# Cross-attention block on one core: the third pair's tokens loaded as rows and turned on TensorE, its queries and keys moved ahead, and another order in the third step

## The chip, the cores and the metric

The kernel runs on one core of one Trainium2 chip. The metric is the device time of one execution in microseconds (us), the median of the runs shown. A profiled execution has a time of its own and, inside it, a span from its first to its last instruction; all times "at 41.05" below count from the start of that span.

## The reference

All values are float32. `x` and the context `c` are 128 sequences of 128 tokens with 256 features; there are 16 heads of 16 features and a hidden layer of 1024.

```
q = x @ Wq + bq ;  k = c @ Wk + bk ;  v = c @ Wv + bv
scores = q k^T / 4 per head, -1e30 where j >= i        (token i sees only j < i)
attn = softmax(scores), row 0 set to zero
x1   = layer_norm(x + (attn v) @ Wo + bo) * ln1_g + ln1_b
out  = layer_norm(x1 + relu(x1 @ W1 + b1) @ W2 + b2) * ln2_g + ln2_b
```

## The kernel before

**Tiles.** The work goes by pairs of sequences: 64 pairs, each 256 tokens. The order of instructions on every engine is the order in which the program writes them (`tc.manual_schedule` for TensorE = PE, VectorE = DVE, ScalarE = ACT, GpSimd = POOL and SyncE = SP). Each engine takes its instructions in that order, so an instruction that waits holds up all behind it on its engine.

**One pair.** `tokens` turns x and c (features onto partitions) on DVE, from tiles that `load` fetched in 32 x 32 blocks. `queries`, `keys` and `values` are the three projections on PE (`pq`, `pk`, `pv`); ACT takes them out of PSUM (`qT`, four instructions for `kT`, `values_out` for `vz` and `vd`). `scores(p, hi)` makes the scores of the upper (`hi` = 1) or lower 64 rows. The softmax runs over three engines: `mask` and the maxima on DVE, the subtraction on POOL (L353), `exponential` on ACT (L360), the sums and reciprocals on DVE (L372, L373), the multiplication on POOL (L374). The attention weights are then turned: on DVE and by 16 DMAs (`turn`, `bring`, into `pT`), or for the first two pairs on PE (`turn_on_pe`, L417, with ACT copying to `pT`, L419). `weigh` multiplies by the values (`pc`), `context` copies on ACT (L456), `attention_out` is the product with Wo (`po`, L463). Then come `attention_sum` (L489), `attention_stats`, the first layer norm `norm1` (for pair 0 on ACT, L505, for the others on DVE, L509), the turning of its result (`turn_x1` through DRAM; for pair 0 `turn_x1_on_pe`, with ACT applying gain and offset, L632, into `x1T`), `hidden` (`ph`, L647, then ACT, L653, into `hT`), `second` (`py`, L665) and the second layer norm.

**Stages.** A prologue, written out by hand (L745 to L806), starts pairs 0 and 1 and makes the projections of pair 2. Pairs 0 and 1 arrive as rows and are turned on PE (`transposed`, four transposes into one PSUM bank); pair 2 is turned on DVE by `tokens(2, "x")` and `tokens(2, "c")`. Then `step(p)` runs for p = 2 to 62: it works on the scores of pair p, the attention output of p - 1, the projections of p + 1, `hidden` of p - 2 and `second` of p - 3. `step(2)` is special: it has a branch of its own, with `turn_x1_on_pe(0)`, `turn_on_pe` for pair 1, `fold_norm1` (L572, products of the first norm's offset with W1, copied by four ACT instructions, L580), and three quarters of `hidden(0, ...)`; the last quarter stands at its end, followed on ACT by eight of the `bring` DMAs. A last part written out by hand ends pairs 61 to 63.

**Buffers.** All of `pv`, `pq`, `pk`, `po`, `ph`, `py`, `pc` and the transposes on PE share four PSUM banks (`ps_1`); a new one waits until the instructions that read an earlier one in its bank are done. The scores have two tiles of their own.

**Queues.** DMAs are issued from SP (loads, the turning through DRAM, half of `bring`) and from ACT (`vd<-vz` in `values_out`, L302, the other half of `bring`, the stores). Every DMA, of whichever queue, takes the next of eight semaphores in the order in which the program writes them, and its issue waits until the DMA that had that semaphore before has landed. The loads at the start stand in the order `load([2, 3])` (eight block DMAs of 128 KB), `w1` (1 MB), three rows, `w2` (1 MB), `load_tokens(1)`, `load([4, 5])`. The functions that the change touches, and their callers:

Of the kernel before, what the change touches and what calls it, by code (L numbers as in the profile page):

```python
# [13 lines left out]
P = 128  # L14
# [5 lines left out]
def tile_cross_attention_block(  # L20
# [59 lines left out]
    def load(ps, both="xc"):  # L80

        n = len(ps)
        for which in both:
            src = x if which == "x" else c
            t = loads.tile(
                [P, KC, n * 2 * NS, 32], F32, tag=f"{which}b{n}", name=f"{which}b_{ps[0]}",
                bufs=n,
            )
            blocks = src[2 * ps[0] : 2 * ps[0] + 2 * n].rearrange(
                "b (i t) (k j f) -> j t k (b i) f", t=32, k=KC, f=32  # L90
            )
            for j in range(NS):
                nc.sync.dma_start(t[32 * j : 32 * j + 32], blocks[j])
            for u, p in enumerate(ps):
                blocks_of[which, p] = t[:, :, u * 2 * NS : (u + 1) * 2 * NS]

    def load_tokens(g, us=slice(0, 4)):
        if g not in tokens_of:
            tokens_of[g] = loads.tile([P, 4, D], F32, tag="x", name=f"x_{g}", bufs=2)
        nc.sync.dma_start(  # L100
            tokens_of[g][:, us], x[4 * g + us.start : 4 * g + us.stop].rearrange("b p d -> p b d")
        )


    def weight(w, name):
        n = w.shape[0] // P
        t = const.tile([P, n, w.shape[1]], F32, tag=name, name=name)
        nc.sync.dma_start(t, w.rearrange("(k p) n -> p k n", p=P))
        return t
# [11 lines left out]
    def row(v, name):  # L121
        t = const.tile([P, v.shape[1]], F32, tag=name, name=name)
        nc.sync.dma_start(t, v.to_broadcast([P, v.shape[1]]))
        return t
# [22 lines left out]
    b1_c = column(b1, "b1_c")  # L147
    g1_c = chunks(ln1_g, "g1_c")
    be1_c = chunks(ln1_b, "be1_c")
    load([2, 3])  # L150
    w1 = weight(W1, "w1")
    g1_r = row(ln1_g, "g1_r")
    be1_r = row(ln1_b, "be1_r")
    b2_r = row(b2, "b2_r")
    w2 = weight(W2, "w2")
    load_tokens(1)
    load([4, 5])
    g2_r = row(ln2_g, "g2_r")
    be2_r = row(ln2_b, "be2_r")
# [152 lines left out]
    def scores(p, hi):  # L312

        st = states[p]
        n = P if hi else HP
        sps = [pair(f"pss{hi}_{p}_{t}") for t in range(2)]
        for m in range(KC):
            for s in range(2):
                first = s * P
                for r in range(NS):  # L320
                    strip = slice(32 * r, 32 * r + 32)
                    nc.tensor.matmul(  # L322
                        sps[r // 2][
                            s * HP : (s + 1) * HP, r % 2, m * 2 * n : (m + 1) * 2 * n
                        ].rearrange("p (e j) -> p e j", e=2),
                        st["qT"][strip, m, first + hi * HP : first + hi * HP + HP],
                        st["kT"][strip, m, :, first : first + n],
                        start=True, stop=True,
                    )
        st["sps", hi] = sps  # L330
        st["sm", hi] = soft.tile(
            [P, H, n], F32, tag=f"sm{hi}", name=f"sm{hi}_{p}", bufs=2
        )
        st["nmx", hi] = small.tile([P, H], F32, tag=f"nmx{hi}", name=f"nmx{hi}_{p}")

    def mask(p, hi, t):
        st = states[p]
        part = slice(t * HH, (t + 1) * HH)
        n = P if hi else HP
        no = neg.rearrange("p u j -> p (u j)") if hi else neg[:, 1, :]  # L340
        nc.vector.tensor_tensor(  # L341
            st["sm", hi][:, part, :].rearrange("p (r n) j -> p r n j", r=2),
            st["sps", hi][t][:, :, : 4 * n].rearrange("p r (n j) -> p r n j", j=n),
            no[:, None, None, :].to_broadcast([P, 2, 4, n]),
            ALU.add,
        )
# [14 lines left out]

    ALL, ONE, TWO = slice(0, H), slice(0, HH), slice(HH, H)

    def sums(p, hi, part):

        st = states[p]
        sm = st["sm", hi]
        n = sm.shape[2]
        su = small.tile([P, H], F32, tag=f"su{hi}", name=f"su{hi}_{p}_{part.start}")
        rs = small.tile([P, H], F32, tag=f"rs{hi}", name=f"rs{hi}_{p}_{part.start}")  # L370
        su, rs = su[:, part], rs[:, part]
        nc.vector.tensor_reduce(su, sm[:, part, :], AX.X, ALU.add)  # L372
        nc.vector.reciprocal(rs, su)  # L373
        nc.gpsimd.tensor_tensor(  # L374
            sm[:, part, :], sm[:, part, :],
            rs[:, :, None].to_broadcast([P, part.stop - part.start, n]), ALU.mult,
        )
# [392 lines left out]
    ps_bv = fold_values()  # L770
    sums(0, 0, ALL)
    scores(1, 1)
    mask(1, 1, 0)
    maximum(1, 1, ONE)
    turn_on_pe(0, 1, range(2))
    add_values(ps_bv)
    values_out(1)
    turn_on_pe(0, 1, range(2, 4))
    mask(1, 1, 1)
    maximum(1, 1, TWO)  # L780
    add_bo(0)
    turn_on_pe(0, 0, range(2))
    tokens(2, "x")
    scores(1, 0)
    exponential(1, 1, ONE)
    weigh(0)
# [1 line left out]
    mask(1, 0, 0)  # L788
    mask(1, 0, 1)
    maximum(1, 0, ALL)  # L790
    tokens(2, "c")
    attention_out(0)
    exponential(1, 1, TWO)
    sums(1, 1, ONE)
    attention_sum(0)
    attention_stats(0)
    shift(0, 1)
    exponential(1, 0, ALL)
    queries(2)
    sums(1, 1, TWO)  # L800
    keys(2)
    norm1(0)
    sums(1, 0, ALL)
    nc.gpsimd.tensor_tensor(be1b_r, be1_r, b2_r, ALU.add)
    values(2)
    values_out(2)  # L806
# [14 lines left out]
    def step(p):  # L821
        nonlocal waiting
        if p > 2:
            load_ahead(p)
        scores(p, 1)
        mask(p, 1, 0)
        maximum(p, 1, ONE)
        if p > 2:
            second(p - 3, 0)
            mask(p, 1, 1)  # L830
            maximum(p, 1, TWO)
            exponential(p, 1, ONE)
            second(p - 3, 1)
            if p + 2 < NP:
                tokens(p + 2, "c")
        else:
            turn_x1_on_pe(0)
            turn_on_pe(1, 1, range(2))
            fold_norm1()
            add_b1()  # L840
            hidden(0, range(FC // 2))
            mask(p, 1, 1)
            maximum(p, 1, TWO)
            exponential(p, 1, ONE)
            low_scores(p)
            turn_on_pe(1, 1, range(2, 4))
            hidden(0, range(FC // 2, 3 * FC // 4))
            turn_on_pe(1, 0, range(2))
            tokens(3, "x")
            add_bo(1)  # L850
        summed = []
        sums(p, 1, ONE)
        exponential(p, 1, TWO)
        if p > 2:
            second_sum(p - 3)
            summed = [p - 3]
        else:
            tokens(3, "c")
            load_ahead(2)
            load_tokens(2)  # L860
            exponential(p, 0, ALL)
        sums(p, 1, TWO)


        weigh(p - 1)
        context(p - 1)
        if p > 2:
            scores(p, 0)
        if p == 3:
            scale_w1()  # L870
            nc.gpsimd.tensor_tensor(b1e_c, b1e_c, b1_c, ALU.add)
        queries(p + 1)
        if p > 2:
            mask(p, 0, 0)
            mask(p, 0, 1)
            maximum(p, 0, ALL)
        if p > 2:
            exponential(p, 0, ALL)
        else:
            sums(p, 0, ALL)  # L880
            add_bo(2)
        turn(p, 1, 0)
        turn(p, 1, 1)
        for q in waiting:
            finish(q)
        attention_out(p - 1)
        attention_sum(p - 1)
        if p > 2:
            sums(p, 0, ALL)
        else:  # L890
            turn(p, 0, 0)
            bring(p, nc.sync, range(NS * NS // 2))
        attention_stats(p - 1)
        if p + 2 < NP:
            tokens(p + 2, "x")
            if p == 2:
                tokens(p + 2, "c")
        if p > 2:
            turn(p, 0, 0)
            bring(p, nc.sync, range(NS * NS // 2))  # L900
        keys(p + 1)
        norm1(p - 1)
        turn_x1(p - 1)
        values(p + 1)
        values_out(p + 1)
        for q in waiting:
            store(q)
        add_bo(p + 1)
        if p == 2:
            residual1(0)  # L910
        residual1(p - 1)
        for q in summed:
            stats(q, states[q]["t2"], 2)
        for q in summed:
            scale_and_shift(q)
        at = NS * NS // 2

        def share(f):
            nonlocal at
            n = NS * NS - at if f == FC - 2 else 0 if f == 0 or p == 2 else NS // 2  # L920
            bring(p, nc.scalar, range(at, at + n))
            at += n

        hidden(p - 2, range(0 if p > 2 else 3 * FC // 4, FC), share)
        for q in summed:
            norm2(q)
        waiting = summed
# [129 lines left out]
```

## Time and profile before

| | |
|---|---|
| median of 3 runs | 1587.57 us (1587.35 to 1588.86) |
| the profiled execution | 1587.7 us |
| its span | 1585.9 us |
| granted TensorE clock, mean | 0.999 |
| busy PE / DVE / POOL / ACT | 99% / 86% / 81% / 48% |
| steady step | 24.27 us (`py` of one step at 112.07, of the next at 136.34) |

How to read it: in a line of the timeline the first number is the start, the second the time from the first start to the last end of the group, then engine, source line, operation, output<-input, shape and count; the brackets give how long the engine idled just before it and what ended that. "SPq" and "ACTq" are DMA issues. Starts are a better measure than durations for PE, since its matmuls overlap: the time a group takes is the distance from its start to the next group's start. Times from the kernel's start to 80 us are the part in which the change lies.

### The profile page before, as it was taken

What the parts mean: (1) busy time and instruction counts of PE and PEld (TensorE: products, weight loads), DVE (VectorE), ACT (ScalarE), POOL (GpSimd) and SP (SyncE); (2) the same over time, 40 slices, a digit from 0 to 9 for tenths busy, and PEclk for the clock granted to TensorE, in tenths of its full rate; (3) what the DMA queues carried; (4) which work ended last, traced back from release to release, by engine and by line L of the source; (5) the groups of instructions that cost most, each with busy time, mean ns of one, the idle gap of its engine ahead of it and who ended that gap; (6) DMA issues with size and microseconds to landing.
All of it is one profiled execution on the core that took longest, in us unless ns stands there. A gap on an engine that the chain in (4) does not pass through costs nothing.

```text
span 1585.9 us, 41280 instructions
## 1 busy us (share of the span) xinstructions
PE 1573.9 (99%) x16514; PEld 1329.4 (84%) x16514; DVE 1369.9 (86%) x1989; ACT 756.8 (48%) x1500; POOL 1281.4 (81%) x1105
## 2 busy tenths in 40 slices
PE   8999999999999999999999999999999999999998
PEld 7788888888888888888888888888888888888887
DVE  7899888888888988898898988888889888889872
ACT  5555445444444454444444444544444455445442
POOL 7878888788887888888888888878888888888883
PEclk9999999999999999999999999999999999999999
DMA  9555665755656556566566565565555655654521
GB/s 199 112 132 127 150 143 121 148 125 133 147 123 144 140 124 159 134 125 147 126 139 146 124 141 138 120 158 130 138 134 126 152 145 123 143 138 108 127 78 34
DMA packets 479935, 210.12 MB, mean 132 GB/s; under 512 B 348672, under 2 KB 448256, under 8 KB 479744
## 3 DMA queue, kind: packets, MB, share of 16 engines
q1 hardware_dynamic: 371104, 134.29, 38.8%
q10 hardware_dynamic: 108640, 73.19, 18.0%
q8 instruction: 131, 2.15, 0.6%
q14 instruction: 60, 0.49, 0.1%
HBM read 70.00 MB, written 33.03 MB: 65 GB/s over the span
## 4 chain that ended last, share of the span: by engine, by line
PE 95%; DMA 1%; DVE 1%; POOL 1%; ACT 1%; SPq 1%; issue 0%; ACTq 0%; POOLq 0%; DVEq 0%
PE ph L647 28%; PE py L665 27%; PE pq L256 7%; PE po L463 7%; PE pk L256 7%; PE pv L288 7%; PE pss L322 6%; PE pc L444 4%; PE pc L434 2%; DMA pT<-tb 1%; SPq L402 0%; POOL sm L374 0%; PE ptp L417 0%; DMA x1t<-tbx 0%; DVE sm L341 0%
## 5 line engine op out<-in xcount | busy, mean ns | idle before, releaser
L353 POOL TENSOR_TENSOR sm<-sm,nmx 128x1024 f32<-128x1024 f32 x192 | 364.3, 1898 | 119.8 <-DVE nmx L352 116.6
L647 PE MATMUL ph<-x1T,w 128*128 128x256 f32 x2048 | 453.4, 380 | 0.0
L665 PE MATMUL py<-w,hT 128*128 128x256 f32 x2016 | 452.8, 383 | 0.3 <-ACT hT L653 0.3
L665 PEld LDWEIGHTS py<-w,hT 128*128 128x128 f32 x2016 | 378.3, 190 | 72.7 <-issue 19.6
L374 POOL TENSOR_TENSOR sm<-sm,rs 128x1024 f32<-128x1024 f32 x192 | 364.2, 1898 | 89.8 <-DVE rs L373 86.2
L647 PEld LDWEIGHTS ph<-x1T,w 128*128 128x128 f32 x2048 | 389.5, 190 | 52.7 <-ACT x1T L632 0.5
L653 ACT ACTIVATE hT<-ph,b1e_c 128x256 f32<-128x256 f32 x504 | 208.6, 471 | 203.0 <-PE ph L647 103.4
L360 ACT ACTIVATE sm<-sm 128x1024 f32<-128x1024 f32 x192 | 200.9, 1054 | 203.9 <-POOL sm L353 203.6
L372 DVE TENSOR_REDUCE su<-sm 128x8 f32<-128x1024 f32 (+1 forms) x192 | 233.6, 1217 | 68.8 <-ACT sm L360 66.7
L341 DVE TENSOR_TENSOR sm<-pss,neg 128x1024 f32<-128x1024 f32 (+1 forms) x256 | 235.1, 939 | 52.4 <-PE pss L322 51.0
L387 DVE STREAM_TRANSPOSE tb<-sm 128x1024 f32<-128x1024 f32 x183 | 220.0, 1227 | 27.9 <-POOL sm L374 27.8
L352 DVE TENSOR_REDUCE nmx<-sm 128x8 f32<-128x1024 f32 (+1 forms) x192 | 234.2, 1220 | 6.6
L542 ACT ACTIVATE t<-t,nb,sd 128x256 f32<-128x256 f32 x124 | 67.7, 593 | 192.3 <-DMA pT<-tb 110.7
L256 PE MATMUL pq<-xT,wq 128*128 128x256 f32 x504 | 125.5, 392 | 0.0
L278 ACT ACTIVATE kT<-pk,bkh,half 128x256 f32<-128x256 f32 x252 | 120.6, 558 | 3.5 <-PE pk L256 3.5
L463 PE MATMUL po<-wo,cxT 128*128 128x256 f32 x512 | 121.1, 380 | 0.7 <-ACT cxT L456 0.7
L288 PE MATMUL pv<-wv,cT 128*128 128x256 f32 x512 | 121.0, 379 | 0.0
L256 PE MATMUL pk<-cT,wk 128*128 128x256 f32 x504 | 119.2, 380 | 0.0
L322 PE MATMUL pss<-kT,qT 32*64 32x256 f32 (+1 forms) x4096 | 116.2, 334 | 0.0
L517 POOL TENSOR_TENSOR x1b<-x,g_r 128x512 f32<-128x512 f32 x64 | 81.5, 1274 | 34.8 <-DVE x L509 34.8
L463 PEld LDWEIGHTS po<-wo,cxT 128*128 128x128 f32 x512 | 97.3, 190 | 13.9 <-ACT cxT L456 0.8
L288 PEld LDWEIGHTS pv<-wv,cT 128*128 128x128 f32 x512 | 97.4, 190 | 13.0
(99 smaller groups left out, 1718.9 us busy)
## 6 DMA issues: line engine op xcount, KB each, us to landing
pT<-tb SPq DMA_DIRECT2D x488, 96.0 KB, 2.9
pT<-tb ACTq DMA_DIRECT2D x488, 96.0 KB, 2.7
out_dram<-t ACTq DMA_DIRECT2D x63, 256.0 KB, 2.5
xb<-in_x_dram SPq DMA_DIRECT2D x124, 128.0 KB, 4.5
cb<-in_ctx_dram SPq DMA_DIRECT2D x124, 128.0 KB, 4.5
x<-in_x_dram SPq DMA_DIRECT2D x31, 512.0 KB, 5.5
x1t<-tbx SPq DMA_DIRECT2D x248, 64.0 KB, 2.3
x1T<-x1t SPq DMA_DIRECT2D x62, 256.0 KB, 3.1
```

The lines of the kernel that those rows point to most:

```text
L256: nc.tensor.matmul(ps[:, m * TP : (m + 1) * TP], w[:, k, m * P : (m + 1) * P], src[:, k, :], start=(k == 0), stop=(k == KC - 1),)
L288: nc.tensor.matmul(pv[:, s * D : (s + 1) * D], st["cT"][:, k, s * P : (s + 1) * P], wv[:, k, :], start=(k == 0), stop=(k == KC - 1),)
L322: nc.tensor.matmul(sps[r // 2][s * HP : (s + 1) * HP, r % 2, m * 2 * n : (m + 1) * 2 * n].rearrange("p (e j) -> p e j", e=2), st["qT"][str ...
L341: nc.vector.tensor_tensor(st["sm", hi][:, part, :].rearrange("p (r n) j -> p r n j", r=2), st["sps", hi][t][:, :, : 4 * n].rearrange("p r ...
L352: nc.vector.tensor_reduce(nmx[:, part], sm[:, part, :], AX.X, ALU.max, negate=True)
L353: nc.gpsimd.tensor_tensor(sm[:, part, :], sm[:, part, :], nmx[:, part, None].to_broadcast([P, part.stop - part.start, n]), ALU.add,)
L372: nc.vector.tensor_reduce(su, sm[:, part, :], AX.X, ALU.add)
L374: nc.gpsimd.tensor_tensor(sm[:, part, :], sm[:, part, :], rs[:, :, None].to_broadcast([P, part.stop - part.start, n]), ALU.mult,)
L387: nc.vector.transpose(st["tb"][:, :, at : at + 256].rearrange("p j (n a) -> p n j a", a=32), st["sm", hi].rearrange("p h j -> p (h j)")[:, ...
L463: nc.tensor.matmul(po[:, s * D : (s + 1) * D], cxT[:, k, s, :], wo[:, k, :], start=(k == 0), stop=(k == KC - 1),)
L647: nc.tensor.matmul(ph[:, i * TP : (i + 1) * TP].rearrange("p (s i a) -> p s i a", s=2, a=32), w1[:, k, (f + i) * P : (f + i + 1) * P], st[ ...
L665: nc.tensor.matmul(st["py"][:, s * D : (s + 1) * D], st["hT"][:, f, s * P : (s + 1) * P], w2[:, f, :], start=(f == 0), stop=(f == FC - 1),)
```

## The change

Pair 2's tokens come as rows (x into `tokens_of[1][:, 0:2]`, c into the new tile `c_third`) and are turned by `turned_on_pe`: four transposes on PE each, and one ACT copy each; the two `tokens(2, ...)` on DVE go. `load([2, 3])` becomes `load([3])`, eight block DMAs of 64 KB, and now stands behind `w1`; its tiles have a tag of their own. `queries(2)` moves between the two halves of `turn_on_pe(0, 1, ...)`; `keys(2)` moves ahead of `attention_out(0)`. `sums` is split so that the DVE part of `sums(1, 1, TWO)` stands ahead of `attention_sum(0)` while its POOL part (`divide`) stays where it was: POOL's order does not change. `exponential(1, 0, ALL)` moves ahead on ACT. In `step(2)` `turn_x1_on_pe(0)` goes behind `turn_on_pe(1, 1, range(2))` and `fold_norm1`; `hidden(0, range(4))` is split in two around `low_scores`, and two of pair 1's transposes move ahead of the third part of `hidden`. From `step(3)` on the order of every engine is that of before.

```diff
-    load([2, 3])
+    load_tokens(1, slice(0, 2))
+    c_third = const.tile([P, 2, D], F32, tag="c_third", name="c_third")
+    nc.sync.dma_start(c_third, c[4:6].rearrange("b p d -> p b d"))
     w1 = weight(W1, "w1")
+    load([3])
...
-    load_tokens(1)
+    load_tokens(1, slice(2, 4))
     load([4, 5])
...
-    def sums(p, hi, part):
+    def sums(p, hi, part, then=True):
...
         nc.vector.tensor_reduce(su, sm[:, part, :], AX.X, ALU.add)
         nc.vector.reciprocal(rs, su)
+        if then:
+            divide(p, hi, part, rs)
+        return rs
+
+    def divide(p, hi, part, rs):
+        sm = states[p]["sm", hi]
+        n = sm.shape[2]
         nc.gpsimd.tensor_tensor(
...
     scores(1, 1)
+
+    def turned_on_pe(p, which, src):
+        st = states.setdefault(p, {})
+        st[which + "T"] = proj.tile([P, KC, TP], F32, tag=which + "T", name=f"{which}T_{p}")
+        pt = transposed(src, f"pt{which}_{p}")
+        nc.scalar.copy(st[which + "T"].rearrange("p k i -> p (k i)"), pt)
+
+    turned_on_pe(2, "x", tokens_of[1][:, 0:2])
     mask(1, 1, 0)
     maximum(1, 1, ONE)
     turn_on_pe(0, 1, range(2))
     add_values(ps_bv)
     values_out(1)
+    turned_on_pe(2, "c", c_third)
+    queries(2)
     turn_on_pe(0, 1, range(2, 4))
     mask(1, 1, 1)
     maximum(1, 1, TWO)
     add_bo(0)
     turn_on_pe(0, 0, range(2))
-    tokens(2, "x")
     scores(1, 0)
     exponential(1, 1, ONE)
     weigh(0)
...
     maximum(1, 0, ALL)
-    tokens(2, "c")
+    exponential(1, 1, TWO)
+    keys(2)
     attention_out(0)
-    exponential(1, 1, TWO)
     sums(1, 1, ONE)
+    rs_two = sums(1, 1, TWO, then=False)
+    exponential(1, 0, ALL)
     attention_sum(0)
     attention_stats(0)
     shift(0, 1)
-    exponential(1, 0, ALL)
-    queries(2)
-    sums(1, 1, TWO)
-    keys(2)
+    divide(1, 1, TWO, rs_two)
+    sums(1, 0, ALL)
     norm1(0)
-    sums(1, 0, ALL)
...
-            turn_x1_on_pe(0)
             turn_on_pe(1, 1, range(2))
             fold_norm1()
             add_b1()
-            hidden(0, range(FC // 2))
+            turn_x1_on_pe(0)
+            hidden(0, range(FC // 4))
             mask(p, 1, 1)
             maximum(p, 1, TWO)
             exponential(p, 1, ONE)
             low_scores(p)
+            hidden(0, range(FC // 4, FC // 2))
             turn_on_pe(1, 1, range(2, 4))
+            turn_on_pe(1, 0, range(2))
             hidden(0, range(FC // 2, 3 * FC // 4))
-            turn_on_pe(1, 0, range(2))
```

## The prediction

> **What bounds the kernel now.** The page comes first: its span, and the share of each engine.
>
> ```profile
> span 1585.9 us, 41280 instructions
> ...
> PE 1573.9 (99%) x16514; PEld 1329.4 (84%) x16514; DVE 1369.9 (86%) x1989; ACT 756.8 (48%) x1500; POOL 1281.4 (81%) x1105
> ```
>
> PE is the bound, and it stands still for only 12.0 us in all. The windows tell where (length, then busy time of PE, PEld, DVE, ACT, POOL, then the granted clock, DMA share, GB/s):
>
> ```profile
> 20.00:80.00 60.00, 55.77 (x718) 44.91 (x717) 53.46 (x71) 36.91 (x72) 52.02 (x37) 1.00 0.68 143
> 80.00:200.00 120.00, 120.00 (x1275) 101.49 (x1274) 108.25 (x156) 58.62 (x116) 98.71 (x84) 1.00 0.61 134
> 200.00:1500.00 1300.00, 1299.11 (x13651) 1098.37 (x13650) 1151.26 (x1661) 620.68 (x1234) 1069.69 (x914) 1.00 0.59 136
> ```
>
> From 80 us to 1500 PE is busy 1419.1 of 1420.0 us, and from `step(3)` on the change leaves every engine's order as it was. So what PE gains or loses before about 73 us moves the whole rest, and nothing else counts. The waits of PE between 20 and 80 us (us in total, times, longest) are what can be won:
>
> ```profile
> PE ptp L417 <- POOL sm L374: 1.8, 3, 0.8
> PE pc L434 <- DMA x1t<-tbx: 0.8, 1, 0.8
> PE pc L434 <- ACT pT L419: 0.7, 2, 0.5
> PE po L463 <- ACT cxT L456: 0.7, 1, 0.7
> ```
>
> By the timeline they stand at 23.23, 25.09 and 26.95 (0.32 + 0.76 + 0.77), 31.08 (0.68), 50.79 and 51.28 (0.53 + 0.18) and 70.64 (0.84): 4.08 us. The name DMA x1t at 70.64 hides the landing of pair 2's last `pT` DMAs.
>
> **What is added to PE.** Eight transposes. Their price is that of the same form for pair 1:
>
> ```profile
> 11.56 0.66 PE L222 MATMUL ptx<-ident,x 128*128 128x128 f32 x4
> 12.05 0.60 PE L222 MATMUL ptc<-ident,c_first 128*128 128x128 f32 x4
> 12.49 1.89 PE L288 MATMUL pv<-wv,cT 128*128 128x256 f32 x8
> ```
>
> From start to start four take 0.49 and 0.44 us: 0.93 for eight. So the most that can be won is 4.08 - 0.93 = 3.15 us, 0.20% of the time. That is just under 0.2%, 3.2 us, which is about what a measurement of this kernel can tell from no change.
>
> **To the product with Wo.** Between `scores(1, 1)` (21.80) and `po` of pair 0, PE now also does the eight transposes (0.93), `pq` (32.91 to 34.64: 1.73) and `pk` (34.64 to 36.37: 1.73): 4.39 us more, against 2.53 us of waits there. With every wait filled `po` would start at 31.08 + 4.39 - 2.53 = 32.94. But new waits come. All these tiles share four PSUM banks, and ACT empties each: the second pair of `ptp` needs the copy of x (done about 24.3), `pq` the first `pT` copy; four further transposes (0.88) then go through before their `pT` copies (two take 0.94 to 0.95, at 26.79 and 41.97) are done, so `weigh(0)` waits about 0.5. I take 1.0 us for these together: `po` at 33.93, 2.85 later than before. Ends: 0 (all banks free in time) and 1.9 (each of four handovers waiting a whole 0.48 us copy).
>
> **From there to `hidden`.** Now `pv` follows `po` directly: PE is ready for what follows 2.85 - 3.46 = 0.61 us earlier than before. But t1 (the sum with x, on DVE) waits for `po`. Before, `po` started at 31.08 and `x1` on ACT at 38.38; DVE's two sums of pair 1 and the statistics lie between, and POOL's order holds a part of it, so of the 2.85 I take 1.0 through: `x1` at 39.4. Ends: 0 (DVE and POOL were the bound, not `po`) and 2.85. ACT's timeline of before shows what follows:
>
> ```profile
> 38.38 1.10 ACT L505 ACTIVATE x<-t,nb,sd 128x256 f32<-128x256 f32 x2
> 39.36 0.65 ACT L298 COPY vz<-pv 128x256 f32<-128x256 f32 x2
> 40.04 0.60 ACTq L302 DMA_DIRECT2D vd<-vz  x1
> 40.68 0.36 ACT L303 COPY vd<-pv 64x256 f32<-64x256 f32 x1 [0.67 <-ACT vz L298]
> 41.05 1.02 ACT L632 ACTIVATE x1T<-ptn,be_c,g_c 128x256 f32<-128x256 f32 x2
> 41.97 1.07 ACT L419 COPY pT<-ptp 128x512 f32<-128x512 f32 x2
> 42.91 1.52 ACT L580 COPY b1s<-ps_b 1x256 f32<-1x256 f32 x4
> 44.45 0.84 ACT L653 ACTIVATE hT<-ph,b_c 128x256 f32<-128x256 f32 x2
> ```
>
> This is the step that decides. ACT is never idle here. From `x1` to `x1T` it takes 2.67 us (38.38 to 41.05), and PE got its first `ph` at 42.29. In the new order the `pT` copies (0.94) and the four `b1s` (1.54) stand ahead of `x1T`: 39.4 + 2.67 + 0.94 + 1.54 = 44.5, the first `x1T` is done some 0.6 later (two take 1.02), and `ph` starts at 45.1, 2.8 us later than before. `turn_x1_on_pe` was put behind `fold_norm1` on PE, which is cheap there, but its reader on ACT went behind that too. PE meanwhile has `ptp`, the 16 products of `fold_norm1` (41.10 to 42.29) and `ptn` (0.5), and idles about 1.25 us ahead of `ptn`, which waits for ACT's `vd` copy to free its bank, and 2.5 us ahead of `ph`.
>
> **To the end of the change.** From the first `ph` PE's work is the same as before, less waits: 0.53 + 0.18 at 51 us go, as pair 1's transposes have moved ahead of a part of `hidden`; `weigh(1)`, 1.95 us from its start at 50.79 to the end of its `pc`, is then back at the 1.49 of `weigh(2)` (70.64 to 72.13), of which 0.18 is the wait counted, so 0.28; and 0.84 at 70.64 goes if the `pT` DMAs are in time. Their second half is issued on ACT behind the last `hT`: before, the last `ph` started at 59.75 and the last of these landed at 69.27, 9.5 later, while SP's issues had to wait for ACT's landings. Now the last `ph` starts about 61.5, so they land by 71.1, and `py`, which takes 7.1 us, ends at about 71.6. This is close; a DMA that takes 3.15 instead of 2.15 us (both are seen there) brings back up to 0.8. Sum: 2.8 - 0.71 - 0.28 - 0.84 = **+1.0 us**. Ends: -2.5 (`x1T` not late at all: 2.8 becomes -0.6) and +4.6 (1.9 for the banks instead of 1.0, all 3.75 of it through to `x1`, so `ph` 1.8 + 3.75 later, and the 0.84 at 70.64 as before: 5.55 - 0.71 - 0.28).
>
> **What costs nothing.** DVE loses two stream transposes of 0.70 us (28.59 and 31.64), and has waits of 1.12 us at 39.38 and 2.46 at 46.71 anyway; its sums of the second half, moved ahead of t1, take 1.4 us and are in the 1.0 above. The rows of x and c are issued at 8.1 and 8.6 in place of the block loads and are wanted at 22.9 and 24.7. The 64 KB blocks of `load([3])` now stand on SP behind `w1`; DVE reads them at 49.2 and 51.2. `w1` itself comes earlier (issued at about 9.1, before at 16.24) and is wanted at 39. `load([4, 5])` and the second half of x move earlier with them.
>
> **Rivals.** *A load in the way of ACT (slower).* Eight semaphores go round over all queues. In the new order the `vd<-vz` of pair 0 on ACT (L302, issued at 15.19) gets the semaphore of the first block of `load([3])`, which on SP stands behind `w1`. Before, the issue of `w1` (SP's timeline) and its time from issue to landing (the DMA view) were:
>
> ```profile
> 16.24 0.74 SPq L108 DMA_DIRECT2D w<-in_L_xattn_W_dram  x1
> ```
>
> ```profile
> w<-in_L_xattn_W_dram SPq DMA_DIRECT2D x1, 1024.0 KB, 7.0
> ```
>
> `w2`, issued at 18.55 among other loads, took 10.2. Loads on SP landed in their order (`w1` 23.20, `w2` 28.75, x 31.35). With 7.0 `w1` lands at 16.1 and the block about 1 us later, near 17.2; ACT has 0.56 us of waiting at 18.57 and 0.45 elsewhere there, so this is nearly free. From 17 on each us is a us, since `kT` of pair 1 (done 21.35) releases `scores(1, 1)` at 21.80. With 10.2 it is 19.3 + 1.2 = 20.5: +3.5 us, in all 1588.6 + 3.5 = 1592.1. Against it: at 9 us few other loads are under way, which is nearer to the 7.0.
>
> *The clock falls.* PE now idles 1.25 and 2.5 us with only 0.5 us of transposes between. The Trainium skill ("TensorE: Matmul & The Clock Gate", What's actually happening) has the clock at half after an idle window of some 3.4 us, and says (Part 4: PE-mode transpose) that transposes do not count as busy; that speaks against this change. The windows at both ends of the trace, same columns:
>
> ```profile
> 3.66:7.07 3.41, 3.33 (x13) 2.50 (x12) 1.41 (x3) 0.16 (x1) 2.85 (x5) 1.00 1.00 311
> ...
> 1584.03:1585.90 1.87, 0.00 (x0) 0.00 (x0) 0.00 (x0) 0.00 (x0) 0.00 (x0) 0.50 0.20 70
> ```
>
> PE's last matmul ended at 1580.56, and the record falls to half at 1584.03, 3.47 us on. In the first line PE did almost only transposes; ones before 7 us took 0.23 each from start to start, later ones 0.11 to 0.12, so they warmed it, or did not stop its warming. A longest single gap of 2.5 us stays under 3.47, so I take no fall. If it falls: at the start PE went at half its later rate from 1.44 to 7.07, 5.6 us, and half of as much is lost again, 2.8 us, in all 1591.4.
>
> *The waits are filled (faster).* `x1T` comes in time, for instance because `x1` is ready much earlier: -2.5 to -3.15 us, 1585.1 to 1584.5, still within 0.2%. Against it stands the order on ACT, which the trace shows without idle time.
>
> **How the numbers follow.** The profiled execution took 1587.7 us, 0.1 above the median of 1587.57; the change is put on the median: 1587.6 + 1.0 = 1588.6. Chances: forecast 0.75 (alone mostly 1586.2 to 1590.8), load in the way 0.13, clock 0.06, waits filled 0.06. The range leaves out the far parts of the last three: 1586.0 to 1591.6. Faster by over 0.2% needs all of 4.08 us filled and a little more: 0.03. Slower by over 0.2% (above 1590.8): most of the load and the clock rivals and the upper end of the forecast: 0.18. Within: 0.79.
>
> **What would show it.** Right: `po` near 33.9, `x1T` behind `b1s` on ACT near 44.5, a wait of 2 to 3 us at the first `ph` released by L632, no wait at 51, the next step's scores of the lower rows at 73.1 (72.13 before). Wrong: an ACT gap at 15 to 20 us at L302 with `scores(1, 1)` past 22; matmuls of `ph` at twice their distance near 45; `ph` at 42.

## The result, and the profile after

The changed kernel takes 1596.85 us (median; 1593.75 to 1598.53) against 1588.21 for the kernel before in the same session: slower by 0.49%, ratio 1.0049 (95% interval 1.0039 to 1.0060). The forecast was 1588.6, and its range ended at 1591.6. The profiled execution took 1598.53 us, the longest of the six, so what is read from it explains that execution and not the median. Its page, answering to the lines of before:

```profile
span 1596.8 us, 41299 instructions
...
PE 1579.3 (99%) x16522; PEld 1330.2 (83%) x16522; DVE 1367.8 (86%) x1987; ACT 756.2 (47%) x1502; POOL 1281.5 (80%) x1105
```

The span is 10.9 us longer, and PE is busy 5.4 us more, although only eight transposes (0.93) were added: some of its work ran slower. The windows say where (second number PE, third from the end the granted clock):

```profile
20.00:80.00 60.00, 51.74 (x563) 39.67 (x561) 43.39 (x56) 33.69 (x69) 43.45 (x32) 0.91 0.58 109
80.00:200.00 120.00, 119.41 (x1271) 100.87 (x1271) 107.12 (x156) 59.62 (x118) 98.18 (x85) 1.00 0.59 138
200.00:1500.00 1300.00, 1298.91 (x13741) 1096.75 (x13740) 1152.11 (x1658) 620.09 (x1229) 1070.37 (x907) 1.00 0.59 135
```

From 20 to 80 us PE loses 8.3 us to waits (4.2 before), and the clock, 1.00 before, is 0.91 on the mean; from 200 to 1500 us PE is as busy as before (1298.91 and 1299.11). The waits of PE in the first 90 us, the costliest first:

```profile
PE ph L657 <- ACT x1T L642: 2.3, 1, 2.3
PE pk L259 <- issue: 2.3, 1, 2.3
PE pss L325 <- ACT kT L281: 1.6, 2, 1.4
...
PE ptn L225 <- ACT vd L306: 1.3, 1, 1.3
PE pc L444 <- issue: 0.4, 1, 0.4
```

The first and the fourth were forecast (2.5 and 1.25). The second and third were not in the sum. PE's timeline (the products alone) and ACT's show what they do:

```profile
33.69 0.48 PE L259 MATMUL pk<-cT,wk 128*128 128x256 f32 x1
36.47 3.27 PE L259 MATMUL pk<-cT,wk 128*128 128x256 f32 x7 [2.30 <-issue]
39.58 1.89 PE L473 MATMUL po<-wo,cxT 128*128 128x256 f32 x8
...
50.68 3.78 PE L657 MATMUL ph<-x1T,w 128*128 128x256 f32 x8 [2.31 <-ACT x1T L642]
```

```profile
14.21 0.65 ACT L301 COPY vz<-pv 128x256 f32<-128x256 f32 x2 [1.15 <-PE pv L291]
18.31 0.73 ACTq L305 DMA_DIRECT2D vd<-vz  x1
19.09 0.36 ACT L306 COPY vd<-pv 64x256 f32<-64x256 f32 x1 [4.23 <-POOL sm L356]
...
45.01 1.09 ACT L515 ACTIVATE x<-t,nb,sd 128x256 f32<-128x256 f32 x2 [2.35 <-POOL nb L538]
46.01 0.62 ACT L301 COPY vz<-pv 128x256 f32<-128x256 f32 x2
46.66 0.60 ACTq L305 DMA_DIRECT2D vd<-vz  x1
47.30 0.36 ACT L306 COPY vd<-pv 64x256 f32<-64x256 f32 x1 [0.67 <-ACT vz L301]
47.57 1.06 ACT L429 COPY pT<-ptp 128x512 f32<-128x512 f32 x2
48.52 1.52 ACT L590 COPY b1s<-ps_b 1x256 f32<-1x256 f32 x4
50.07 1.02 ACT L642 ACTIVATE x1T<-ptn,be_c,g_c 128x256 f32<-128x256 f32 x2
```

Three things are to be seen. ACT sits at L305 from 14.9 to 18.3: the first rival of the prediction. (The profile names POOL's L356 for the idle time, but `vd` waits for no such thing; the first block of `load([3])`, issued at 9.46, is what the issue waited for, as the runs with that load moved show.) Seven products of `pk` take 3.11 us to the start of `po`, against 1.73 for eight at full clock, and eight of `ph` 3.71. And from `x1` to `x1T` ACT takes 5.06 us, as forecast (5.15). The windows of 3.41 us round the slow stretches:

```profile
32.76:36.17 3.41, 1.41 (x71) 1.02 (x59) 3.27 (x5) 1.91 (x3) 3.41 (x4) 0.99 0.75 111
36.17:39.58 3.41, 3.11 (x8) 2.52 (x8) 0.77 (x2) 0.00 (x0) 1.88 (x2) 0.51 0.94 145
...
46.40:49.81 3.41, 0.72 (x8) 0.42 (x4) 3.15 (x3) 2.67 (x8) 3.41 (x4) 0.99 0.22 38
49.81:53.22 3.41, 2.54 (x6) 2.09 (x7) 0.00 (x0) 1.25 (x3) 3.41 (x2) 0.50 0.15 13
53.22:56.63 3.41, 3.41 (x38) 2.16 (x38) 1.00 (x2) 1.78 (x3) 0.10 (x1) 0.50 0.96 145
```

The clock is at half for one such window from 36.1 and for two from 49.8, each time after a window in which PE was busy less than half the time. All edges lie on one grid of 3.41 us; they stand some 0.05 us earlier than these windows, and by them the two windows before the falls hold 1.46 and 0.76 us of work.

### The profile page after: what moved, and what is told of

Same layout as the page of the kernel before. It is cut to its first block, busy times and chain, and to the rows that moved or that the text cites. A ratio compares the mean times of both kernels' runs of the same rounds, so it can differ in the third digit from the quotient of the medians.

```text
span 1596.8 us, 41299 instructions
## 1 busy us (share of the span) xinstructions
PE 1579.3 (99%) x16522; PEld 1330.2 (83%) x16522; DVE 1367.8 (86%) x1987; ACT 756.2 (47%) x1502; POOL 1281.5 (80%) x1105
## 4 chain that ended last, share of the span: by engine, by line
PE 93%; DVE 2%; DMA 1%; ACT 1%; SPq 1%; POOL 1%; issue 1%; ACTq 0%; POOLq 0%; DVEq 0%
PE ph L657 27%; PE py L675 26%; PE pq L259 7%; PE po L473 7%; PE pk L259 7%; PE pv L291 6%; PE pss L325 6%; PE pc L454 3%; PE pc L444 2%; DMA pT<-tb 1%; SPq L412 1%; DVE su L375 0%; DVE sm L344 0%; DVE nmx L355 0%; ACT sm L363 0%
## 5 line engine op out<-in xcount | busy, mean ns | idle before, releaser
L356 POOL TENSOR_TENSOR sm<-sm,nmx 128x1024 f32<-128x1024 f32 x192 | 364.2, 1897 | 116.2 <-DVE nmx L355 116.0
L259 PEld LDWEIGHTS pk<-cT,wk 128*128 128x128 f32 x504 | 96.5, 192 | 16.1 <-issue 2.8
```

Source lines behind the costliest of these rows:

```text
L259: nc.tensor.matmul(ps[:, m * TP : (m + 1) * TP], w[:, k, m * P : (m + 1) * P], src[:, k, :], start=(k == 0), stop=(k == KC - 1),)
L356: nc.gpsimd.tensor_tensor(sm[:, part, :], sm[:, part, :], nmx[:, part, None].to_broadcast([P, part.stop - part.start, n]), ALU.add,)
```

## The experiments

The start of the kernel scatters from run to run: the first `pk` takes 1.83 us in most profiles, but 2.1 to 2.4 in before, cover and best2, and 3.6 in ring, fill and quiet. So places are counted from pair 1's first transposes (11.56 in before, 11.29 in after). The last column is where the change ends. The profiles late and quiet are left out, since in them a later wait of PE (6.18 and 9.30 us) falls into the stretch.

| profile | scores(1,1) | gap at `pk` | `po` | first `ph` | `ph` to end | scores(3,0) |
|---|---|---|---|---|---|---|
| before | 10.24 | 0 | 19.52 | 30.73 | 29.84 | 60.57 |
| after | 11.75 | 2.30 | 28.29 | 39.39 | 31.47 | 70.86 |
| after2 | 11.35 | 2.29 | 27.93 | 39.16 | 31.53 | 70.69 |
| ring | 10.24 | 0 | 22.26 | 33.36 | 30.27 | 63.63 |
| fill | 10.24 | 0.90 | 23.42 | 34.53 | 28.69 | 63.22 |
| x1f | 11.42 | 0.54 | 24.72 | 34.05 | 28.60 | 62.65 |
| both | 10.24 | 0.44 | 22.95 | 32.29 | 28.68 | 60.97 |
| cover | 10.24 | 0.63 | 23.67 | 33.01 | 28.69 | 61.69 |
| ringfill | 10.24 | 1.15 | 23.67 | 34.78 | 28.66 | 63.44 |
| step2_only | 10.24 | 0 | 19.53 | 32.62 | 28.98 | 61.60 |
| best2 | 10.24 | 0.53 | 23.05 | 31.80 | 28.69 | 60.49 |
| best3 | 10.24 | 0.33 | 23.37 | 32.12 | 28.66 | 60.78 |

**Blocks ahead of w1 (ring).**

```diff
-    w1 = weight(W1, "w1")
     load([3])
+    w1 = weight(W1, "w1")
```

> Theory: the vd<-vz of pair 0 on ACT waits for the landing of the first block of load([3]), which stands behind w1. With load([3]) ahead of w1 that block lands near 13, the issue goes out near 15 (18.31 in the changed kernel), kT of pair 1 is done near 21.4 and scores(1, 1) start near 21.8 instead of 23.04: 1.7 us less on PE, all else as in the changed kernel, 1595.1. Rival: kT of pair 1 is late for another reason (the exponentials behind POOL), scores(1, 1) stay at 23 and the time at 1596.8.

1592.77 us, ratio 1.0033 (1.0021 to 1.0045). scores(1,1) is back at 10.24, and the gap at `pk` is gone too, which was not expected; the run's start was 1.8 us late, though, so that ACT might not have met the wait in any case (fill, with after's load order and the same late start, did not). The runs both, ringfill and best2 with their ordinary starts settle it: the issue goes out at 14.6 to 15.5 and scores(1,1) never wait. This trace also holds the forecast's own order nearly alone: `po` 2.74 us later than before (forecast 2.85), `ph` 2.63 (forecast 2.8). The clock still fell, for one window:

```profile
46.78 2.66 PE L657 MATMUL ph<-x1T,w 128*128 128x256 f32 x8 [2.31 <-ACT x1T L642]
```

**Loads of pairs 4 and 5 late (late).**

```diff
-    load([4, 5])
...
             add_b1()
+            load([4, 5])
```

> Theory: the 2.30 us at 34.17 in which PE waits for nothing shown is its own instruction fetch, held up by the eight 128 KB block DMAs of load([4, 5]), and the half clock after it comes from that gap. With load([4, 5]) issued only behind add_b1 (near 47) the DMA engines are quiet at 33: no such gap, no half clock at 36, 2.3 + 1.6 = 3.9 us less, 1592.9. Rival: the gap comes of the instructions themselves (so many short ones ahead of it), whatever the DMA engines do: it stays, 1596.8; pair 4's blocks may then only be later.

1600.72 us, ratio 1.0080 (1.0067 to 1.0093). The late loads push the next ones (`xb` of pairs 6 and 7, 55.6 to 72.2 on SP) ahead of pair 2's `pT`, and PE waits 6.18 us at `weigh(2)`. The gap at `pk` was 0.82 and the clock did not fall there, but the other versions, with those loads in place, had 0.33 to 1.15, so this run says neither. At that time `w2` and x were still under way.

**The waits filled (fill).**

```diff
+            pf = pair("pf"); fillers(pf, 0, 3)
             turn_x1_on_pe(0)
+            fillers(pf, 1, 5)
```

> Three extra products (into a free PSUM tile, used for nothing) ahead of the transposes of x1 and five behind them fill the two waits of PE (1.26 and 2.31 us). Theory: the half clock from 49.8 to 56.6 comes of these waits; with PE busy the clock stays full there, ph of pair 0 goes at its usual distance, 3.0 us less: 1593.8. The waits themselves stay, since x1T comes when it did. Rival: the clock falls for another reason (it goes on from the fall at 36, or transposes): 1596.8 and half clock near 50 as before.

1595.15 us, ratio 1.0046 (1.0033 to 1.0058); the profiled execution took 1593.56. The clock is full throughout, and with products in both waits `ph` goes at its usual distance:

```profile
47.74 2.02 PE L657 MATMUL ph<-x1T,w 128*128 128x256 f32 x8
```

From `ph` to the end it is 28.69 us against 31.47: 2.8 us is what the second fall cost. The whole gained only 1.7 by the medians, 0.5 by the ratios, where 3.0 were expected; the trace has a further wait of PE for nothing shown (0.64 at the next `pq`), which the extra instructions may have brought.

**x1 turned first again (x1f).**

```diff
+            turn_x1_on_pe(0)
             turn_on_pe(1, 1, range(2))
             fold_norm1()
             add_b1()
-            turn_x1_on_pe(0)
```

> turn_x1_on_pe(0) back at the head of step 2, all else as changed. Theory: the order on ACT (two pT copies and four b1s copies ahead of x1T) makes x1T 2.5 us late and with it the first ph; that wait goes, and the half clock after it (3.0): 5.5 us less, 1591.3. Rival: x1T is late because x1 is, behind po; then ph moves by less than 0.5 us and the time stays near 1596.

1590.82 us, ratio 1.0021 (1.0012 to 1.0030): 6.0 us less than the changed kernel by the medians, 4.4 by the ratios (0.28% of 1588), 5.5 expected. That it came near is in part luck: by the traces scores(3,0) come 8.21 us earlier, but 3.57 of them stand ahead of `po`, where the edit changes no order (a smaller gap at `pk`, and no fall of the clock there); 4.64 lie behind it. There is no wait ahead of `ph` and no fall; PE waits 1.4 us for `x1` instead, ahead of `ptn`. The order on ACT was the cause, not `x1`.

**Both edits (both).**

> load([3]) ahead of w1 and turn_x1_on_pe(0) back at the head of step 2. Theory: beyond the order itself three costs were left out of the forecast: ACT's wait for the first block (1.3 to 1.7), PE's wait for its own instructions (0.5 to 2.3, gone in the run with load([3]) ahead of w1, where the instruction fetch was recorded 17.1 us after pair 1's first transposes instead of 20 to 22.5), and the half clock. None is left here; the run with the order alone undone stood at +2.1 us by the trace, less 1.3 and 0.5: +0.2 us on before, 1587.8. Rival: the wait for instructions depends on PE's order alone and stays; then +0.8 or more and a gap at the second product of pk.

1590.22 us, ratio 1.0013 (1.0004 to 1.0021); the profiled execution, 1588.23, stands at +0.40 by the trace. The ACT wait is gone, the clock full, but 0.44 us of the gap at `pk` stayed, as the rival had it: the loads' order alone does not remove it. The median lies 2.4 us above the expectation, and the trace does not show why.

**The forecast's own case (ringfill).** ring and fill together.

> load([3]) ahead of w1, and the eight extra products that keep PE busy through its two waits, the changed order kept. This is what the forecast had: new order, no ACT wait at L305, full clock. Theory: +1.0 of the forecast and 0.4 for the pT that come late at weigh(2): +1.4 us on before, 1589.0, with ph of pair 0 starting 2.6 to 2.8 us later than before, counted from pair 1's first transposes. Rival: the order itself costs more than the sum says; then over +2.5 us with full clock and no gap at pk.

1594.26 us, ratio 1.0043 (1.0029 to 1.0056): a miss by 5 us, so that no run shows the forecast's case as a time. Up to the end of the change the trace is as the theory has it but for the gap, 1.15 us: `ph` +4.05 (2.8 + 1.15 = 3.95), scores(3,0) +2.87. Yet the span is 6.6 us longer than before's. Of what comes later, 0.68 is a wait at `pq` as in fill, and from 90 to 1480 us PE stands idle 2.5 us instead of 0.9. The rest was not found. So a kernel with extra instructions is no clean measure of the whole time here; its trace up to 75 us is.

**The third step alone (step2_only).** The prologue of before with the changed branch of `step(2)`.

> The prologue of before with the third step of the changed kernel. Theory: x1T stands behind pT and b1s on ACT, 1.9 to 2.5 us late; later waits give 1.4 back: +0.5 us with a full clock; with a gap of some 2.3 us ahead of ph the clock falls for one or two windows of 3.4 us and takes 1.7 to 3.0 more: +2.2 to +3.5, 1589.8 to 1591.1. Rival: the fall of the clock needs the prologue's shorter or longer waits too; then full clock and 1588.1.

1589.20 us, ratio 1.0011 (1.0002 to 1.0020), from 1587.63 (the profiled one) to 1593.45. `ph` came 1.89 us later, 0.86 was given back, scores(3,0) +1.03. In this profile the clock stayed full though PE waited 2.06 us ahead of `ph`; so a gap of this size does not always make it fall. The gap (41.53 to 43.59) was cut by an edge of the grid at 42.16, and the window behind that edge still held 1.99 us of work.

**A quiet start (quiet).** Both edits, with `w2`, half of x, `load([4, 5])` and two rows behind `add_b1`.

> As both edits together (load([3]) ahead of w1, turn_x1 at the head of step 2), with w2, the second half of x, load([4, 5]) and two rows issued only behind add_b1, so that the DMA engines are idle from about 25 to 45 us; only the profile up to pair 1's weigh is read, later these loads are in the way. Theory: PE's wait for its instructions (0.44 us there, at the second product of pk) is an instruction fetch that starts when PE has done some 214 matmuls and is late behind queued loads; with quiet engines it is recorded at most 0.5 us after that point and the gap is gone. Rival: the fetch is not held up by loads; its time and the gap stay.

No gap at `pk`; the single time, 1603.02, holds a later wait of 9.3 us for `pT`. The time at which PE's instruction fetch (queue q8 in the DMA view) is recorded fits all profiles. The view does not name the engine: q8 has 131 packets in a run, one for every 252 of PE's 16522 matmuls and as many weight loads, and that it is PE's is read from this. In quiet and ring the fetch comes 0.3 us after PE's 214th matmul; take that as the point where it is asked for. The fetches of the changed kernel (33.8 to 33.9) and of quiet (30.5 to 30.6):

```profile
q8 instruction: 1, 0.02, 65.1%
```

```profile
q8 instruction: 1, 0.02, 59.6%
```

| profile | 214th matmul | fetch | 345th (two ahead of `pk`) | gap ends |
|---|---|---|---|---|
| before | 28.2 | 31.4 | 34.2 | no gap |
| after | 30.3 | 33.8 | 33.5 | 36.47 |
| after2 | 29.8 | 33.0 | 33.1 | 36.03 |
| x1f | 29.9 | 31.2 | 33.2 | 34.39 |
| both | 28.0 | 29.3 | 31.3 | 32.34 |
| late | 29.4 | 31.3 | 32.7 | 34.18 |
| quiet | 30.2 | 30.5 | 33.5 | no gap |
| ring | 30.4 | 30.7 | 33.7 | no gap |

The gap always ends 2.5 to 3.2 us after the recorded fetch, and always at the second product of `pk`; the later waits at `pq` in fill and ringfill end 2.7 and 2.5 us after a fetch too. Before, PE took 6.1 us from the 214th matmul to the 345th; in the new order, where only transposes, scores and `weigh` lie between, 3.3. Before had a fetch late by 3.2 us and hid it, with less than 1 us to spare. So the shorter stretch is what laid the wait open. That the wait is for the fetch is argued from these times; no run removed the fetch alone. Why the fetch is late by 0.3 in ring and by 1.3 and 1.9 in both and ringfill, with loads under way in all three, stays open. That loads hold it up fits quiet, but quiet also began late, as ring did, and ring had no gap with the loads in place; so it is not proved.

**Longer products in that stretch (cover).** Both edits, and:

```diff
-    queries(2)
     turn_on_pe(0, 1, range(2, 4))
...
     scores(1, 0)
+    queries(2)
```

> As both edits together, with queries(2) moved from between the transposes to behind scores(1, 0): the same instructions, but 1.7 us of long products stand in the stretch between the fetch's start and the point where PE runs out. Theory: the gap at pk (0.44) goes though the loads are the same; transposes may wait up to 0.5 for POOL instead, so the time is within 0.5 us of both edits alone. Rival: the gap depends on the loads only and stays.

1589.05 us, ratio 1.0003 (0.9994 to 1.0012). The gap stayed, 0.63. PE's time from the 214th matmul to the 345th grew to 3.9 only: counted in matmuls, the eight long products took the place of eight short ones in the stretch, and two waits of 0.3 in all went from it. The fetch was late by 2.1, and a transpose waited 0.8 for a bank, so `po` came 0.72 later than in both. A miss: the edit moved too little of the stretch.

**Two versions meant to beat both kernels (best2, best3).** best2 is both, with `fold_norm1` and `add_b1` ahead of `norm1(0)`; best3 adds the edit of cover.

> load([3]) ahead of w1, turn_x1_on_pe(0) at the head of step 2, and fold_norm1 with its four copies ahead of norm1(0), where ACT idles 2.3 us and PE 1.4 us in the run with only turn_x1 put back. Theory: first ph 0.7 us later than before, then 1.2 to 1.4 back: -0.6 us on before, 1587.0, no more than can just be seen. Rival: the copies on ACT push x1 back and nothing is won: 1587.8 as with the two edits alone.

> The version with fold_norm1 ahead of norm1(0), and queries(2) behind scores(1, 0). Theory: the gap of 0.53 at pk goes; by the trace the version before it stood 0.1 us under before when counted from pair 1's first transposes, so -0.6 us or so, 1587.0. Rival: a wait of the transposes for POOL takes the gap's place, 1587.6 or a little more.

best2 1589.66 us, ratio 1.0007 (0.9999 to 1.0016); best3 1588.86, 1.0007 (0.9998 to 1.0016). PE's waits for `x1` and `x1T` fell from 1.6 us (both) to 0.9, and the trace of best2 stands 0.08 under before's, but neither is faster. In best3 0.33 us of the gap at `pk` stayed, and a transpose waited 0.8. The medians lie 0.9 to 2.0 us above before's (1587.65 and 1587.99 in the two sessions), more than their traces show; this remainder was not traced.

**The changed kernel again (after2).**

> The changed kernel once more, for a second profile. Theory: ACT waits at L305 (1.0 to 1.7 us on scores(1, 1)) unless the start of the kernel is late by the slow clock; PE waits for instructions at the second product of pk by 0.5 to 2.5 us, whatever it is in this run; the clock falls for one or two windows after the wait for x1T. 1594 to 1598. Rival: the 2.3 us and the two falls belonged to the one profiled execution; then the clock is full and the time 1591 or less.

1595.03 us, ratio 1.0043 (1.0029 to 1.0057). The same gap, the same two falls, the same place; here the profiled execution, 1596.96, is again the longest:

```profile
36.03 3.36 PE L259 MATMUL pk<-cT,wk 128*128 128x256 f32 x7 [2.29 <-issue]
```

Of all ten runs of this kernel, those with a mean clock of 0.998 took 1593.75 to 1595.26 us, those with 0.996 or 0.997 1596.46 to 1598.53. That fits one window at half clock more or less; no profile of the faster ones was kept.

## Why the prediction was wrong

**The sum of the order itself held.** By ring `po` came 2.74 us later, `x1` on ACT 0.86, and the first `ph` 2.63 (2.85, 1.0 and 2.8 forecast); from `x1` to `x1T` ACT took 5.07 (5.15). So the step that the prediction called decisive was right. From `ph` to the end every profile of the changed `step(2)` with the changed prologue and full clock needs 28.60 to 28.69 instead of 29.84, so 1.18 come back where 1.83 were forecast: 0.35 to 0.44 of the difference is a wait "issue" inside `weigh(2)`. In the changed kernel PE goes on there at 80.78, 0.09 us after the last of pair 2's `pT` DMAs landed (80.69). That one went out on ACT only at 78.60, since SP's DMA before it on the same semaphore landed at 78.58, 3.12 us after its issue; the times are alike in ring. The prediction had taken the 0.84 at 70.64 as gone, and had said that a DMA of 3.15 us would bring part of it back. The other 0.2 was not found. Order alone: 2.63 - 1.18 = +1.45, against +0.97. This is put together from several profiles, and no run shows it by itself.

**Three costs came on top**, and they add up to the place where the change ends. Counted from pair 1's transposes the changed kernel is 10.29 us late at scores(3,0):

- ACT's wait at L305: scores(1,1) start 1.51 late and take 0.47 longer, as `kT` arrives in parts: 1.98.
- PE's wait for instructions at `pk`: 2.30.
- Half clock: `pk` lasts, without the gap, 1.76 longer than in ring (5.89 - 2.30 - 1.83), and `ph` to the end 2.80 longer: 4.56.

1.45 + 1.98 + 2.30 + 4.56 = 10.29. Pair 1's transposes themselves came 0.27 earlier, and the span is 10.9 longer: 0.8 more were lost later and were not traced.

**The steps that failed.** First, the rival "a load in the way of ACT" was named with its place and taken as free, from `w1` in 7.0 us and a block 1 us later: 17.2. `w1` took 9.1 us (7.5 and 8.4 in fill and late, with the same order), the issue went out at 18.31, and from 17 on it cost about what the text said, 1 us per us. With load([3]) ahead of `w1` it is gone. It was weighed at 0.13; every profile with that load order shows it (`scores(1,1)` 0.6 to 1.5 us late), except fill, which began late. The landing of `w1` in the changed kernel, in the DMA view:

```profile
w<-in_L_xattn_W_dram SPq DMA_DIRECT2D x1, 1024.0 KB, 9.1
```

Second, the step that turned `pk` from 34.64 to its new place asked only for data, banks and engines. It did not ask whether PE would have its instructions. Before's page had a row for this, q8 instruction, and waits named "issue"; that the fetch came at 31.4 and PE went past its 345th matmul at 34.2 was there to be read in before's trace, but no rival was made of it. The runs showed 2.30 us there, and with it the first fall of the clock (1.76).

Third, the clock. The text let it fall only after a single gap near 3.47 us, the one fall that before's trace shows, and gave it 0.06. What the runs show is a share of a fixed window: falls came after windows of 3.41 us with PE busy 0 to 1.46 us, none after windows with 1.47 or more (1.47 at the end of cover, from 1580.58; 1.55 in quiet, 1.83 in x1f, 1.99 in step2_only, 2.03 in ring). The profile models the ends of matmuls, so these shares are not exact. So a gap's place on the grid counts as well as its length. In the changed kernel the gap of 2.3 at `pk` lay mostly in one window, and gaps of 1.26 and 2.31 shared another in part. In ring the gap of 2.31 alone, nearly whole in the window from 44.61, left 1.24 and did it. A gap of 2.17 in quiet, cut by an edge, did not:

```profile
54.64:58.05 3.41, 1.55 (x7) 1.43 (x8) 3.21 (x5) 1.44 (x3) 2.24 (x2) 1.00 0.82 99
```

The Trainium skill ("TensorE: Matmul & The Clock Gate", What's actually happening) states a free-running window of about 3.4 us; the grid agrees with that. Its one idle window as the condition is not what happened here: the windows before both falls held 1.46 and 0.76 us of work. The price of a fall, 2.8 us, met the second one (2.80, two windows) in part by luck: it was taken from the start of the kernel, and the fall at `pk`, of one window, cost 1.76. There were two falls.

So two of the three rivals came true at once, beside a cost that none of them named. They were treated as alternatives, of which one might come, while the wait for the late `x1T`, a part of the forecast itself, led to one of them (the clock).

## What to carry to other kernels

Where PE is full, a new wait of 2 us can cost more than itself, because the clock may follow: count what PE does in a window of 3.4 us, not the single gap. When instructions are reordered, look for stretches of many short ones, and set the time they take against how late the instruction queue's fetches come. When a load moves in a queue, follow its semaphore to the next engine that will need it, and price that with the slowest landing of the trace.

## What was not expected of the hardware

- PE's instruction fetch was recorded up to 3.6 us after PE's 214th matmul, where in the earliest runs it came 0.3 us after it, and PE's waits ended 2.5 to 3.2 us after the fetch. PE took 131 matmuls in 3.3 us there.
- The granted clock goes by a grid of 3.41 us whose edges lie alike, within 0.2 us, in both profiles of the changed kernel (falls at 36.1 and 49.8 in the first). It fell after windows with PE busy 1.46 us or less and held after windows with 1.47 or more; at half clock it did not come back after a window with 2.5 us of work, but did after one with 3.1.
- Filling waits with products whose results nobody uses held the clock, but the kernel was hardly faster for it (ratio 1.0046, against 1.0049).
